# First attention of a six-stage transformer block: score banks, bank of sums and the planner's costs

## The chip, the cores and the metric

The kernel runs on one core of a Trainium2 chip. A core has TensorE (PE, matmuls and transposes), ScalarE (ACT), VectorE (DVE), GpSimd (POOL) and SyncE (SP), which here only issues transfers. Each takes its own instructions strictly in order and waits on semaphores for the others. Matmuls write to PSUM: eight banks, each of 512 f32 values in each of 128 partitions. All other tiles lie in SBUF. The metric is the device time of one execution in microseconds (us); less is better.

## The reference

The input is four sequences of 1024 tokens with 128 features. Six sublayers follow, each added to the stream (half of it for the feed-forward kind):

```python
x = L0_attn_x
x = x + 0.5 * _L0_ffn_ref(_layernorm(x), ...)
x = x + _L0_attn_ref(_layernorm(x), ...)
x = x + 0.5 * _L0_ffn_ref(_layernorm(x), ...)
x = x + 0.5 * _L1_ffn_ref(_layernorm(x), ...)
x = x + _L1_attn_ref(_layernorm(x), ...)
x = x + 0.5 * _L1_ffn_ref(_layernorm(x), ...)
```

The change rewrites the schedule of `_L0_attn_ref`, an attention by distance with 16 heads of 8 features whose queries, keys and values are one projection:

```python
Q = (x @ W_k.T).reshape(B, S, H, dk).transpose(0, 2, 1, 3)
sq_norm = jnp.sum(Q * Q, axis=-1, keepdims=True)
dot = jnp.einsum('bhsk,bhtk->bhst', Q, Q)
squared_dist = sq_norm - 2.0 * dot + sq_norm.transpose(0, 1, 3, 2)
attn = softmax(-squared_dist * inv_sqrt_dk)
context_q = jnp.einsum('bhst,bhtk->bhsk', attn, Q)
```

`_L0_ffn_ref` is a two-layer feed-forward with gelu. `_L1_attn_ref` is a causal attention with 16 heads of 64 features. `_L1_ffn_ref` is itself two layers, each a local attention (8 heads, windows of 64 tokens, normalised and rotated queries and keys) and a gated feed-forward; it runs twice.

## The kernel before

The six stages are recorded as `ffn0a`, `attn0`, `ffn0b`, `ffn1a`, `attn1`, `ffn1b`. Each stage hands the planner small steps with `at(t, f)`: a step is a function that issues a few instructions, and `t` a rough due time. Nothing is issued at once. `Plan.run` first calls every step in recording mode, in which `issue` notes each instruction's engine, its `cost` and the tiles it touches. `prepare` builds the dependences, `order` then places all steps by their ready times and priorities (it keeps one free time for each engine), and `latest` walks back from the end to give each step a new priority. `best_order` does this six times and keeps the order with the earliest end. The steps are then issued for good in that order, and `follow` ties each engine's instructions to it. Hence a changed cost in the planner can move instructions in every stage. All instructions of the kernel are issued from one line of `issue`, so every row of the profile says L237.

Names of the trace: `wordsP` is PSUM, `wordsS`, `wordsR` and `words` are parts of SBUF. A PSUM tile is asked for with `plan.bank(tag, slots, ...)`: the slots are bank numbers at which it may begin, and a tag's tiles take them in turn.

**The first attention** (`attn0`) works on units `(b, g, c)`: batch `b` (4), group `g` of four heads (4), block `c` of 128 keys (8), and for each unit the two halves `k` of 512 queries and the two pairs `p` of heads.

- `prep` prepares half a batch: layer norm, `turn` (four f32 transposes), `project` (rounded matmuls in three parts), a split of Q into three bf16 parts (`part1` to `part3`, `square`, `norm`, `spread`), and `turn_q` / `keep_q`: eight bf16 transposes into a bank and two DVE copies out of it. Batch `b + 1` is prepared while batch `b` is attended.
- `score(n)`: two matmuls with 64 rows each into a place of two banks (1024 f32 columns); two places, banks 0-1 and 2-3.
- `exp(n)`: one ACT exponential over the 1024 columns into a tile `e`, of which there are six. There are 512 of them in the stage.
- `weigh(j)`: four matmuls that add the exponentials, times Q and a column of ones, into a bank of sums; four heads lie in it 32 partitions apart. Each is f32 and runs as two passes, which stand as two records in the trace. Query half 0 has bank 4, half 1 bank 5.
- `collect`: one DVE copy of a bank of sums to SBUF after the eighth key block.
- `finish`: per half batch, transposes of the sums (`turn_c`), the division, a transpose (`turn_n`), the output projection and the add to `x`.

Bank 6 serves `turn`, `project` and half of `turn_q`; bank 7 the other half of `turn_q` and all of `finish`.

**The local attention** (`ffn1`, twice, two layers each, 32 tiles of 128 tokens per layer) matters too, since the planner may move its steps. Per tile: `project` (three f32-rounded matmul groups), DVE rotations (`turn_a`, `turn_b`), POOL additions (`add`), `sums` (a DVE reduction of the squares), `clip`, ACT `log` and `guess`, DVE `newton`, POOL `normalise`, PE `turn` of q and k, `score`, DVE `top` (two row maxima), eight ACT `exp`, DVE `inverse`, POOL `norm_e`, PE `turn_e`, ACT `untwist_e`, PE `weigh`, `project_out`. Steps of several tiles are interleaved. **The second attention** (`attn1`) has an order of the same kind.

## Time and profile before

| | us |
|---|---|
| median of 3 runs (3216.11 to 3220.35) | 3218.98 |
| the profiled execution | 3219.6 |
| its span | 3217.8 |
| first to last exponential of the first attention, start to start | 508.7 |
| mean granted TensorE clock, share of full speed | 0.984 |

The stages follow one another on PE with little overlap: the first exponential of the first attention starts at 87.96 us, the last at 596.64; the local attention's first scores are at 681.0; the second attention's first scores at 1402.3; the second local attention's first scores at 2500.2; the last matmul at 3212.4.

The costliest groups of the first attention, by shape (count, then busy time and mean length of one, then idle time of its engine just before):

```profile
L237 ACT ACTIVATE wordsS<-wordsP 128x1024 f32<-128x1024 f32 x512 | 485.7, 1028 | 23.2 <-PE wordsP L237 20.7 <-ACT wordsS L237 0.7
L237 PE MATMUL wordsP<-wordsS 64*128 64x512 bf16 x1022 | 194.4, 384 | 17.0 <-ACT wordsS L237 9.0
L237 DVE COPY words<-wordsP 128x512 f32<-128x512 f32 x32 | 22.1, 690 | 87.4 <-PE wordsP L237 87.4
```

These are the exponentials, the scores and the copies of the sums. A matmul's length in the trace is modelled and overlaps the next, so what it costs is read from the distance between starts.

### The profile page before, as it was taken

Reading aid. Unit: us, or ns where it says so; the run is one execution under the profiler, and the core shown is the slowest. Engines: PE = TensorE matmul, PEld = TensorE weight load, DVE = VectorE, ACT = ScalarE, POOL = GpSimd, SP = SyncE. Lnnn points to the kernel's source line nnn. Section 1 sums busy time; section 2 is a strip of 40 time slices with the busy share of each in tenths; the row PEclk is TensorE's granted clock in tenths of the full one; section 3 lists DMA queues with packets and bytes.
Section 4 is the critical chain, followed back from the end, with each engine's and each line's share of the span. In section 5 each row is a group of like instructions: output and inputs, shape, how many; then the busy total and the mean of one; then the engine's idle time right before and its main releaser. Section 6 shows DMA issues by size and latency. Waiting matters only on the chain.

```text
span 3217.8 us, 76341 instructions
## 1 busy us (share of the span) xinstructions
PE 3029.4 (94%) x27082; PEld 2134.7 (66%) x27108; DVE 2192.4 (68%) x6641; ACT 2467.9 (77%) x6856; POOL 1451.3 (45%) x1621
## 2 busy tenths in 40 slices
PE   8999999989998999899999999999999899999978
PEld 6322222567776777677777777777777677777767
DVE  8433341467867676778788778878787777676774
ACT  6999999768868687657777777767777788686873
POOL 1000000079958585523333333333343898585870
PEclk9999999999999999899999999999999999999989
DMA  1000000022212221122222222212231322222211
GB/s 40 1 1 1 1 3 11 21 68 63 57 40 58 44 56 35 42 57 49 47 55 45 46 50 45 52 44 47 54 80 34 76 54 56 44 53 49 55 42 30
DMA packets 209427, 137.31 MB, mean 43 GB/s; under 512 B 148548, under 2 KB 164632, under 8 KB 209048
## 3 DMA queue, kind: packets, MB, share of 16 engines
q1 hardware_dynamic: 208328, 131.87, 18.1%
q8 instruction: 217, 3.56, 0.5%
q14 instruction: 162, 1.33, 0.1%
q0 software_dynamic: 720, 0.56, 0.1%
HBM read 17.58 MB, written 2.10 MB: 6 GB/s over the span
## 4 chain that ended last, share of the span: by engine, by line
PE 58%; ACT 16%; DVE 13%; issue 5%; POOL 5%; DMA 1%; SPq 1%; DVEq 0%; ACTq 0%; POOLq 0%
PE wordsP L237 58%; ACT wordsS L237 12%; DVE wordsS L237 8%; POOL wordsS L237 3%; ACT words L237 3%; DVE words L237 3%; POOL words L237 1%; SPq L237 1%; DVE wordsP L237 1%; DVE wordsR L237 1%; DMA wordsS<-wordsS 1%; ACT wordsR L237 0%; DMA words<-words 0%; ACT wordsP L237 0%; DMA wordsS<-L_attn_x 0%
## 5 line engine op out<-in xcount | busy, mean ns | idle before, releaser
L237 PE MATMUL wordsP<-wordsS 128*128 128x128 f32 (+8 forms) x12062 | 1657.9, 331 | 114.2 <-POOL wordsS L237 44.1
L237 ACT ACTIVATE wordsS<-wordsP,wordsS 128x128 f32<-128x128 f32 (+4 forms) x1952 | 921.6, 495 | 335.7 <-PE wordsP L237 204.1
L237 PEld LDWEIGHTS wordsP<-wordsS 128*128 128x128 f32 (+3 forms) x10296 | 926.0, 145 | 329.4 <-POOL wordsS L237 85.3
L237 POOL TENSOR_SCALAR wordsS<-wordsS 128x128 f32<-128x128 f32 (+7 forms) x630 | 476.1, 758 | 678.6 <-DVE wordsS L237 484.5
L237 PE MATMUL wordsP<-wordsR 128*128 128x512 f32 (+2 forms) x2592 | 718.9, 409 | 13.6 <-ACT words L237 4.1
L237 POOL TENSOR_TENSOR wordsS<-wordsS 128x512 f32<-128x512 f32 (+1 forms) x512 | 532.6, 1053 | 430.2 <-DVE wordsS L237 411.4
L237 ACT COPY wordsS<-wordsP 128x512 f32<-128x512 f32 (+4 forms) x1040 | 543.8, 541 | 170.6 <-PE wordsP L237 160.7
L237 DVE TENSOR_REDUCE wordsS<-wordsP 128x1 f32<-128x512 f32 (+4 forms) x1024 | 576.9, 582 | 70.6 <-PE wordsP L237 64.1
L237 PE MATMUL wordsP<-wordsS,words 128*64 128x64 f32 (+3 forms) x6216 | 524.0, 299 | 34.6 <-DVE words L237 12.6
L237 ACT ACTIVATE wordsS<-wordsP 128x1024 f32<-128x1024 f32 (+3 forms) x646 | 516.8, 863 | 27.1 <-PE wordsP L237 22.7
L237 PEld LDWEIGHTS wordsP<-wordsR 128*128 128x128 f32 (+1 forms) x2592 | 451.1, 191 | 115.2 <-ACT words L237 10.2
L237 PE MATMUL wordsP<-words 128*128 128x512 f32 (+3 forms) x1540 | 414.7, 375 | 13.0 <-DMA words<-W_vT 10.9
L237 ACT ACTIVATION_READ_ACCUMULATOR wordsS<-wordsP,wordsS 128x1 f32 x1792 | 397.2, 222 | 0.0
L237 DVE COPY wordsS<-wordsP 128x512 f32<-128x512 f32 (+4 forms) x444 | 238.8, 551 | 219.0 <-PE wordsP L237 213.5
L237 PEld LDWEIGHTS <-wordsS 64*128 64x128 bf16 (+1 forms) x1792 | 117.7, 95 | 390.3 <-issue 373.1
L237 PEld LDWEIGHTS wordsP<-wordsS,words 128*64 128x64 f32 (+2 forms) x5704 | 302.6, 136 | 101.5 <-issue 48.1
L237 DVE TENSOR_TENSOR wordsS<-wordsP,wordsS 128x256 f32<-128x256 f32 (+3 forms) x560 | 252.7, 463 | 161.5 <-PE wordsP L237 122.8
L237 DVE TENSOR_TENSOR words<-wordsP,wordsS 128x256 f32<-128x256 f32 (+1 forms) x448 | 227.8, 527 | 133.4 <-PE wordsP L237 87.9
L237 PEld LDWEIGHTS wordsP<-words 128*128 128x128 f32 x1540 | 247.6, 192 | 44.1 <-DMA words<-W_kT 10.9
L237 PEld LDWEIGHTS wordsP<-words,wordsS 64*64 64x64 f32 (+1 forms) x4672 | 186.8, 142 | 79.4 <-issue 54.3
L237 PE MATMUL wordsP<-words,wordsS 64*64 64x128 f32 (+1 forms) x4672 | 227.3, 279 | 8.0 <-POOL words L237 3.1
L237 ACT ACTIVATE words<-wordsP,wordsS 128x512 fp32r<-128x512 f32 (+1 forms) x192 | 131.0, 689 | 69.8 <-PE wordsP L237 67.9
(62 smaller groups left out, 2219.7 us busy)
## 6 DMA issues: line engine op xcount, KB each, us to landing
words<-words SPq DMA_DIRECT2D x648, 128.0 KB
wordsS<-words SPq DMA_DIRECT2D x88, 128.0 KB
wordsS<-wordsS SPq DMA_DIRECT2D x48, 128.0 KB
wordsS<-wordsS SPq DMA_DIRECT2D x48, 112.0 KB
wordsS<-c_rot SPq DMA_DIRECT2D x16, 256.0 KB
wordsS<-L_attn_x SPq DMA_DIRECT2D x8, 256.0 KB
words<-wordsS SPq DMA_DIRECT2D x16, 128.0 KB
out_dram<-wordsS SPq DMA_DIRECT2D x8, 256.0 KB
```

Of the source, the lines that this page charges most:

```text
L237: self.follow(engine, getattr(engine.engine, name)(*args, **kw))
```

## The change

The change has two parts.

In the first attention, the units become `(b, g, k, c)`: a query half runs through all eight key blocks before the other begins. Then only one bank of sums is in use (bank 7, tag `a0.acc`), and it is copied out every eighth `weigh` as before. The scores get a third place (banks 4-5), and everything of `prep` and `finish` that used bank 7 shares bank 6, under one tag.

```diff
-            W["acc", k] = plan.bank(f"a0.acc{k}", [4 + k])
+            W["acc"] = plan.bank("a0.acc", [7])
...
-                pb = V["pb", K, u, z] = plan.bank("a0." + "mn"[z], [6 + z], (128, 1024), BF)
+                pb = V["pb", K, u, z] = plan.bank("a0.m", [6], (128, 1024), BF)
...
         def score(n):
-            (b, g, c), k, p = units[n // 4], n // 2 % 2, n % 2
-            sc = V["s", n] = plan.bank("a0.s", [0, 2], (128, 2, 512))
+            (b, g, k, c), p = units[n // 2], n % 2
+            sc = V["s", n] = plan.bank("a0.s", [0, 2, 4], (128, 2, 512))
...
-            ve.tensor_copy(V["cu", b][:, g, 512 * k : 512 * k + 512], W["acc", k])
+            ve.tensor_copy(V["cu", b][:, g, 512 * k : 512 * k + 512], W["acc"])
...
-                pc = V["pc", K, u] = plan.bank("a0.n", [7], (128, 16, 32))
+                pc = V["pc", K, u] = plan.bank("a0.m", [6], (128, 16, 32))
...
-        units = [(b, g, c) for b in range(self.B) for g in range(4) for c in range(8)]
-        N = 4 * len(units)
+        units = [(b, g, k, c) for b in range(self.B) for g in range(4) for k in range(2) for c in range(8)]
+        N = 2 * len(units)
```

`merge3`, `turn_n` and `output` move from `a0.n` to `a0.m` in the same way.

In the planner, the estimates change. A matmul's cost now depends on the part of the array that it uses, a switch of that part between two matmuls is charged, a change of ACT's table is charged, steps that use the SBUF port common to DVE and POOL are kept apart in the estimate, and a transfer takes longer to issue and to land.

```diff
+    TABLE = 1.3
...
+    def mode(name, args):
+
+        if name == "transpose":
+            return 128, 128, False
+        tile = lambda n: 32 if n <= 32 else 64 if n <= 64 else 128
+        return tile(args[1].shape[0]), tile(free_size(args[1])), args[1].dtype == FR
+
+    def switch(self, old, new):
+
+        if old is None or old[:2] == new[:2]:
+            return 0.0
+        return 0.2 if any(m == (64, 128, True) for m in (old, new)) else 0.1
+
+    def port(self, key, name, out, ins):
+
+        if key == "G":
+            return True
+        psum = lambda x: x.tensor.name in self.owner and self.owner[x.tensor.name].space == "P"
+        if key != "D" or psum(out) or any(psum(x) for x in ins):
+            return False
+        if name in ("tensor_tensor", "scalar_tensor_tensor"):
+            return True
+        return name in ("tensor_scalar", "tensor_copy") and free_size(out) > 1
...
-                t = 4 * free_size(x) / 2400
+                t = 4 * free_size(x) / 2400 + 0.009
+            elif x.dtype == FR:
+                t = max(free_size(x) / 2400 + 0.015, 0.112)
             else:
-                t = max(free_size(x) / 2400, 0.107 if x.dtype == FR else 0.056)
-            row = math.prod(out.tensor.shape[1:])
-            return 0.04 if free_size(w) <= 64 and out.offset // row else t + 0.004
+                t = free_size(x) / 2400 + 0.003
+
+            return t * mode[0] * mode[1] / 128**2
...
+            if s.table is not None and s.table != table:
+                t, table = max(t, free[z]) + self.TABLE, s.table
...
+                if e == "P":
+                    t, mode = t + self.switch(mode, m), m
...
+                if port:
+                    for a, b in taken_port["G" if e == "D" else "D"]:
+                        if a <= t < b:
+                            t = b
+                    taken_port[e].append((t, t + cost))
                 if e == "S":
-                    free[e] = t + 0.6
+                    free[e] = t + 0.74
                     dma = max(dma, t + 1.25) + max(cost, 0.18)
-                    end = dma + 0.96 - self.X_LAT
+                    end = dma + 1.96 - self.X_LAT
```

When a step takes its PSUM or SBUF place, all tags that share a cell with any of its tag's slots (`g.peers`) are woken, not only those of the slot taken. `latest` uses the same 0.74 for SyncE. No instruction of the other stages is added, removed or altered; they may stand in another order.

## Prediction

> **What bounds the kernel now.** I read the busy shares first, then a table by stage, then single instructions in the stage that the change rewrites, then who waited for whom.
>
> ```profile
> span 3217.8 us, 76341 instructions
> ...
> PE 3029.4 (94%) x27082; PEld 2134.7 (66%) x27108; DVE 2192.4 (68%) x6641; ACT 2467.9 (77%) x6856; POOL 1451.3 (45%) x1621
> ```
>
> TensorE (PE) looks like the bound, but ends of matmuls are modelled, so the stages decide. The rows below are the first attention, a first layer and part of a second layer of the local-attention block, and the middle of the second attention; the columns after the length are busy time of PE, weight loads, VectorE (DVE), ScalarE (ACT), GpSimd (POOL), then granted clock and DMA.
>
> ```profile
> 88.00:597.00 509.00, 488.85 (x3734) 135.88 (x3732) 161.06 (x480) 487.68 (x522) 3.26 (x3) 1.00 0.01 3
> 667.00:920.00 253.00, 231.93 (x2631) 179.40 (x2634) 195.18 (x589) 205.23 (x744) 216.10 (x219) 0.99 0.27 60
> 994.00:1150.00 156.00, 144.27 (x1590) 115.95 (x1593) 106.96 (x310) 117.01 (x415) 108.39 (x109) 0.99 0.23 51
> 1500.00:2400.00 900.00, 893.91 (x6665) 686.92 (x6663) 724.40 (x2127) 662.55 (x1899) 329.81 (x451) 1.00 0.23 51
> ```
>
> The second attention is full of matmuls (893.91 of 900). The local-attention layers fill no engine. In the first attention PE and ACT are both near 96%, so I went to single instructions, ACT and then PE.
>
> ```profile
> 262.01 2.85 ACT L237 ACTIVATE wordsS<-wordsP 128x1024 f32<-128x1024 f32 x3
> 265.10 3.77 ACT L237 ACTIVATE wordsS<-wordsP 128x1024 f32<-128x1024 f32 x4 [0.23 <-PE wordsP L237]
> ```
> ```profile
> 262.76 0.62 PE L237 MATMUL wordsP<-wordsS,words 128*128 128x128 bf16 x8
> 263.31 3.30 PE L237 MATMUL wordsP<-wordsS 64*128 64x512 bf16 x24
> 266.54 0.62 PE L237 MATMUL wordsP<-wordsS,words 128*128 128x128 bf16 x8
> 267.09 1.36 PE L237 MATMUL wordsP<-wordsS 64*128 64x512 bf16 x10
> ```
>
> One exponential is 1.02 us and a free run of them starts one every 0.915 us ((3.77 - 1.02) / 3 = 0.917, (2.85 - 1.02) / 2 = 0.915). From 263.31 to 266.54 PE did four pairs of score matmuls and two groups of sums (24 records): 3.23 us for four exponentials, 0.81 each. A block of eight transposes then adds 0.55. So ACT is the slower engine by 0.1 us each, unless other PE work comes between. The first exponential starts at 87.96 and the last at 596.64: 508.7 us for 511 steps. At 0.915 they would be 467.6, so **41.1 us of ACT's time is lost** inside this stage. In the list of single instructions a score starts 0.05 us after the exponential that frees its place, and that place's exponential can start 0.49 us after the score. With two places the next exponential (0.915) covers that with 0.915 - 0.54 = 0.37 us to spare. A group of sums holds PE 0.94 us (0.414 to its second pass, 0.525 to the score after it), so PE is late again and again; in no case of a late exponential was the score waiting for its place.
>
> ```profile
> PE wordsP L237 <- POOL wordsS L237: 44.4, 49, 5.2
> PE wordsP L237 <- ACT wordsS L237: 36.7, 90, 2.1
> PE wordsP L237 <- DVE wordsS L237: 28.3, 30, 7.7
> PE wordsP L237 <- DVE words L237: 16.9, 12, 6.4
> ```
>
> PE's own waits over the whole span: the largest, 44.4 us, is for GpSimd's normalised weights, which are turned (`turn_e`) in the local-attention layers. Followed back in a second layer:
>
> ```profile
> 1216.53 1.02 DVE L237 TENSOR_TENSOR wordsS<-wordsP,wordsS 128x512 f32<-128x512 f32 x2 [0.24 <-ACT words L237]
> ...
> 1217.73 1.23 DVE L237 TENSOR_REDUCE wordsP<-words 128x16 f32<-128x1024 f32 x1
> 1218.87 0.68 DVE L237 TENSOR_REDUCE wordsS<-wordsP 128x4 f32<-128x512 f32 x1
> ```
> ```profile
> 1219.65 0.37 ACT L237 ACTIVATE wordsS<-wordsP,wordsS 128x128 f32<-128x128 f32 x1 [1.10 <-DVE wordsS L237]
> ```
>
> Here the scores' last matmul started at 1216.4, yet their row maximum (0.68) began at 1218.87, behind a `sums` of 1.23 us for a later tile; ACT stood idle 1.10 us for it. Over 56 tiles of the second layers the median delay from scores to maximum is 1.7 us, from scores to `turn_e` 8.85, while PE's own order holds 7.6 us of work between the two.
>
> **The change, part by part.** The trace ran 3219.6 us (span 3217.8 and 1.8 around it), 0.6 above the median 3218.98; the sum is made against 3219.6.
>
> *Three score places.* One more exponential covers PE: its spare lateness grows from 0.37 to 0.37 + 0.915 = 1.29 us. I ran a sum along the scores in the order they stand: PE's work since the last score (from rows as above) minus 0.915, never below nothing, and what passes the spare time is ACT's loss. For the order before with 0.37 it gives a loss of 53 us where 41.1 is measured, so it overstates by a quarter. For the order of the changed kernel with 1.29 it gives 9.4. PE has 445 us of work between first and last score in both orders, below 467.6, so ACT stays the bound. 467.6 + 9.4 = 477, and 2 for what follows: 479, **-30 us** (508.7 - 479). Bounds: -41 if nothing is lost; -19 if four copies of sums come late as they did before (3.6, 3.2, 4.4 and 4.6 us after the last matmul, against 0.66) and PE, which now has one bank, stands for 3 us each.
>
> *One bank of sums.* Each of 32 groups of (batch, four heads, query half) ends in a copy of the bank, and the next group's first matmul waits. From the last sums matmul's start: 0.66 to the copy, 0.69 for it, 0.07 back: 1.42. Behind that wait on PE stand the scores, then ACT. The new order puts 0.89 to 1.33 us of scores and transposes behind the last pass of 0.52 us, 1.41 to 1.85 in all, except six groups with 0.92; five of these are in the last batch, where PE has only 22 of 29.3 us of work per 32 exponentials and loses nothing. Hidden; without this cover 32 x 0.9 = 29 us. "PSUM — Partial Sum Buffer" of the Trainium skill, section "PSUM bank collisions raise a hardware error", says that two engines must not use one bank at once, so matmuls cannot run on into the next group during the copy; this speaks against one bank, and by it with no filling the three places would gain about nothing. The new order fills the gap, so I side with the rows.
>
> *One bank for preparing and finishing.* `turn_q` and `finish` give up bank 7. A block's two reading copies (0.42 each, 0.34 apart) free the bank 1.0 us after its last transpose; the order leaves 1.3 to 1.7 us at all but four places (at most 1 us short each). 0, at worst +3.
>
> *The planner.* Counted along the two orders, switches of the array's row and column split are 1500 before and 1495 after; one costs 0.525 - 0.414 = 0.11 us, so -0.5. Table loads are 18 and 18. SyncE keeps 619 of 644 steps in order, and PE never waits for a transfer after the start, so the longer transfers are worth 0. PE's work summed along either order is the same within 0.3 us. In the second attention the order differs but PE has no more work and little idle: 0, within 5 either way. For the common port the trace has one row of weight:
>
> ```profile
> 440.51 3.11 DVE L237 TENSOR_TENSOR words<-words 128x64 f32<-128x64 f32 x1
> ```
>
> The same operation takes 0.45 at 444.01; GpSimd ran two additions of 1.27 from 440.99 to 443.5, and this one ended just after them. This loss (2.7 us) can go; it is within the bounds above.
>
> *What the planner moves in second layers.* There the order of PE and GpSimd is unchanged. VectorE's differs: the maxima stand before `sums` and one of the rotations, 1.2 us earlier by VectorE's own work, and three exponentials stand before the copies of the tile before. That can take up to the 44.4 us of PE's wait for GpSimd. The other end: `sums` now comes 1.3 us later (two maxima of 0.6 to 0.68), and its tile's normalising could become late: 64 tiles x 1.3 = +83 if all of it showed, but it stood before a wait of 1 to 2 us for ACT, so I take +20 as the far end. Nearest is the row with a wait really seen; but behind it stand waits of 36.7 and 28.3 us that take its place: a third, **-15**. First layers: GpSimd is 216 of 253 us busy, 0.
>
> Sum: 3219.6 - 30 - 0.5 - 15 = 3174, said as **3175**.
>
> **Rivals.** *The first attention alone*: the waits in the local layers only change hands. 3219.6 - 30 = 3190. For it: four waits of like size stand behind one another. Against: the maximum is plainly queued behind work that nobody needs yet. *Both in full*: nine tenths of 41.1 and five sixths of 44.4, -37 each: 3146. For it: the second layers fill no engine (PE 144 of 156 modelled, 7.5 us of work in a tile of 9.0). Against: it needs every other wait to stay covered. *Slower, by the late `sums`*: in the local layers `sums`, the logarithm, `newton` and `normalise` of a tile come after its neighbour's maxima; if GpSimd then starts `normalise` late, the turning of q and k waits in all 128 tiles. It decides from 30 / 128 = 0.23 us a tile; at 0.4 it gives 3219.6 - 30 + 51 = 3241. For it: GpSimd is the fullest engine of the first layers. Against: GpSimd's order hardly moved. *It does not do what it says*: one bank of sums takes back what the third place gives, 29 of 30, and the planner moves nothing: 3219.
>
> **How the numbers follow.** Forecast 0.45, first attention alone 0.22, both in full 0.16, slower 0.11, nothing 0.06. About 0.2% (6.4 us) is what can be told from no change. Faster holds the first three and a little of the last: 0.84; same 0.05; slower 0.11. The range runs from 3142 (both in full) to 3212 (the late copies, +5 in the second attention, and some loss in the local layers); the forecast's own is 3160 to 3190.
>
> **What would show it.** The exponentials' first to last start should fall to about 479 us and ACT's wait for PE there below 10; the copies of sums should start 0.66 us after the last matmul in nearly all groups. The switches and PE's summed work stay. In second layers the median from scores to maximum should fall below 1 us, and PE's wait for GpSimd from 44 to some 25. I am wrong if PE is seen waiting for VectorE at the 32 group ends, or if waits for `turn` of q and k grow by as much as those for `turn_e` fall.

## The result, and the profile after

The changed kernel takes 3224.76 us (3220.54 to 3229.07) against 3218.98 (3215.11 to 3222.05) beside it on the same chip: a ratio of 1.0018, 95% interval 1.0011 to 1.0026. It is 0.18% slower: the interval leaves out 1, but the step is smaller than the 0.2% that the prediction took as what can be told from no change. 1.4% less was forecast.

The busy shares of the changed kernel say nothing of it; every engine has what it had before:

```profile
span 3220.4 us, 76369 instructions
...
PE 3017.7 (94%) x27108; PEld 2127.8 (66%) x27108; DVE 2181.8 (68%) x6640; ACT 2460.3 (76%) x6856; POOL 1453.2 (45%) x1621
```

So again by stages. The rows of the changed kernel are: the first attention from its first to its last exponential, the first local-attention block from its first to its last score, the seam from there to the first score of the second attention, the second attention from first to last score, and the second local block likewise. Columns as before, after the length: PE, weight loads, DVE, ACT, POOL, granted clock, DMA share and GB/s.

```profile
88.60:580.90 492.30, 479.34 (x3756) 129.94 (x3756) 162.31 (x479) 478.87 (x525) 3.27 (x3) 1.00 0.01 3
666.20:1330.90 664.70, 605.72 (x6842) 481.94 (x6845) 477.57 (x1425) 515.46 (x1861) 494.77 (x498) 0.97 0.23 52
1330.90:1393.40 62.50, 51.72 (x350) 41.61 (x343) 45.20 (x149) 28.38 (x69) 13.51 (x23) 0.91 0.20 47
1393.40:2469.70 1076.30, 1065.11 (x7924) 819.02 (x7922) 855.62 (x2535) 792.55 (x2275) 394.10 (x538) 1.00 0.22 50
2494.70:3148.80 654.10, 584.26 (x6675) 464.27 (x6675) 462.34 (x1405) 503.66 (x1844) 495.04 (x499) 0.96 0.23 51
```

The same stages took 508.7, 665.9, 55.4, 1073.7 and 646.5 us before. The seam and the second local block of the kernel before, whose rows stand nowhere above:

```profile
1346.90:1402.30 55.40, 48.76 (x350) 39.76 (x343) 43.56 (x147) 28.27 (x69) 13.52 (x23) 0.98 0.21 49
2500.20:3146.70 646.50, 583.65 (x6666) 461.94 (x6675) 465.35 (x1407) 503.77 (x1849) 494.76 (x499) 0.96 0.23 52
```

The first attention gives 16.4; the seam takes 7.1, the second attention 2.6 and the second local block 7.6. What the first attention gained was lost again in stages that the diff does not touch, and the seam's clock, 0.98 before, is 0.91. PE's waits over the whole span did not shrink but changed hands (44.4 for POOL, 36.7 for ACT and 28.3 for DVE before):

```profile
PE wordsP L240 <- POOL wordsS L240: 50.6, 44, 5.2
PE wordsP L240 <- DVE wordsS L240: 34.4, 30, 6.8
PE wordsP L240 <- DVE words L240: 22.5, 19, 7.4
PE wordsP L240 <- POOL words L240: 22.3, 14, 6.5
PE wordsP L240 <- ACT wordsS L240: 19.5, 41, 1.9
```

**A second layer of the changed kernel.** In single instructions, the place that answers to the one shown before:

```profile
1198.69 1.10 PE L240 MATMUL wordsP<-words,wordsS 64*64 64x128 f32 x32
...
1200.21 0.68 DVE L240 TENSOR_REDUCE wordsS<-wordsP 128x4 f32<-128x512 f32 x1
...
1201.67 0.68 DVE L240 TENSOR_REDUCE wordsS<-wordsP 128x4 f32<-128x512 f32 x1
...
1202.46 1.23 DVE L240 TENSOR_REDUCE wordsP<-words 128x16 f32<-128x1024 f32 x1
1202.53 1.59 ACT L240 COPY wordsS<-wordsP 128x512 f32<-128x512 f32 x3
...
1204.43 0.44 ACT L240 ACTIVATE wordsS<-wordsP,wordsS 128x128 f32<-128x128 f32 x1
```
```profile
1207.25 1.04 POOL L240 TENSOR_TENSOR wordsS<-wordsS 128x512 f32<-128x512 f32 x1 [1.66 <-DVE wordsS L240]
```

Both maxima of the tile (0.68) now run before `sums` (1.23), the first 0.4 us after the last score: the move the prediction read from the order took place. But ACT then copies four banks of other tiles (1202.53 to 1204.6) before the second half's exponentials, and `inverse` of that half stands on DVE at 1207.00 behind two rotations; so POOL gets its input late and PE turns the weights as late as before. Over the 56 tiles the median from scores to the first maximum fell from 1.7 to 0.14 and 0.19 us in the two blocks, and from scores to `turn_e` it stayed (8.85 before, 8.85 and 8.88).

**One bank of sums.** 28 of the 32 copies of the bank start 0.66 us after the last matmul's start (four at 1.21 to 1.76), and the next group's first matmul starts 0 to 0.67 us after the copy's end. That step held.

**Where the first attention still loses.** 24.7 us are left above the 467.6 of a free run. In windows of 32 exponentials (29.28 at 0.915 each) the first takes 35.6 and those at the three changes of batch 33.2 to 34.0: together 19.2 too many. At the first two changes of batch ACT waits 3.1 us each for PE, and PE is not standing but busy with other matmuls (33.11 of 33.50 us, 33.06 of 33.20). At the third ACT waits only 0.6 us and has nine other instructions of its own between the exponentials. The first and the third change:

```profile
213.00:246.50 33.50, 33.11 (x250) 9.96 (x249) 17.76 (x58) 30.39 (x33) 0.00 (x0) 1.00 0.00 1
460.00:494.00 34.00, 34.00 (x256) 10.48 (x254) 15.09 (x59) 33.26 (x43) 0.00 (x0) 1.00 0.00 1
```

Counted in the trace between one exponential's start and the next, about 16 of the 24.7 us pass while ACT waits for a busy PE, 6 go to other instructions of ACT and 3 pass while PE stands idle. (PE's ends are modelled, so the split is rough.) The largest single loss, in the first window, is one where PE stands:

```profile
99.31 0.69 DVE L240 CAST wordsR<-wordsP 128x512 fp32r<-128x512 f32 x1
...
100.03 0.69 DVE L240 TENSOR_TENSOR wordsR<-wordsP,wordsR 128x512 fp32r<-128x512 f32 x1
...
100.78 0.55 PE L240 MATMUL wordsP<-wordsR 128*128 128x128 f32 x3 [2.59 <-DVE wordsR L240]
...
101.75 1.02 ACT L240 ACTIVATE wordsS<-wordsP 128x1024 f32<-128x1024 f32 x1 [1.80 <-PE wordsP L240]
```

PE stands 2.59 us at a projection of the next batch whose input DVE splits late; the score that ACT needs is queued behind it (101.26). A third place covers a PE that is busy 1.29 us too long, not one that stands for 2.59.

**The common port.** The planner now counts it, yet the one heavy case of before (3.11 us at 440.51) is there unchanged in the changed kernel:

```profile
425.44 3.14 DVE L240 TENSOR_TENSOR words<-words 128x64 f32<-128x64 f32 x1
```
```profile
425.93 2.51 POOL L240 TENSOR_TENSOR wordsS<-wordsS 128x512 f32<-128x512 f32 x2
```

"SBUF — State Buffer" of the Trainium skill, section "SBUF: two separate sides", calls the pair that DVE and GpSimd share an exclusive lock that the first comer holds for its whole instruction. The row fits a loser that stands still: DVE ends 0.14 us after the second addition. But DVE began 0.49 us before the first addition and waited out both; GpSimd had been issuing a transfer since 425.14, so the row does not settle who came first.

**The seam.** PE, DVE and POOL of the changed kernel where the seam first loses time:

```profile
1358.30 2.42 DVE L240 SCALAR_TENSOR_TENSOR wordsS<-wordsS 128x4 f32<-128x4 f32 x2
```
```profile
1358.16 2.54 POOL L240 TENSOR_TENSOR wordsS<-wordsS,words 128x512 f32<-128x512 f32 x2 [5.11 <-DMA wordsS<-wordsS]
```
```profile
1363.62 0.96 PE L240 MATMUL wordsP<-wordsR 128*128 128x512 f32 x3 [3.00 <-DVE wordsS L240]
1365.37 1.65 PE L240 MATMUL wordsP<-wordsR 128*128 128x512 f32 x3 [0.78 <-DVE wordsS L240]
```

and the granted clock there (the third number from the end of each row):

```profile
1363.00:1366.00 3.00, 1.60 (x5) 1.02 (x6) 2.92 (x16) 0.00 (x0) 0.00 (x0) 0.85 0.00 0
1366.00:1369.00 3.00, 2.22 (x6) 1.30 (x5) 2.21 (x9) 0.00 (x0) 0.00 (x0) 0.50 0.00 0
1369.00:1372.00 3.00, 3.00 (x10) 2.15 (x9) 1.48 (x5) 0.94 (x5) 2.12 (x5) 0.51 0.32 44
```

Two DVE steps on 4 elements (0.16 us each elsewhere) take 2.42 while POOL adds, then statistics of another tile stand ahead of the copy that PE needs. PE idles 3.00 us, the clock falls to 0.50 for six microseconds, and the same three matmuls take 1.65 instead of 0.96. This order pays for its hole twice; the last section shows that the hole's length alone does not decide it.

### The profile page after: what moved, and what is told of

It reads as the page before. It is cut to its first block, busy times and chain, and to the rows that moved or that the text cites. A ratio compares the mean times of both kernels' runs of the same rounds, so it can differ in the third digit from the quotient of the medians.

```text
span 3220.4 us, 76369 instructions
## 1 busy us (share of the span) xinstructions
PE 3017.7 (94%) x27108; PEld 2127.8 (66%) x27108; DVE 2181.8 (68%) x6640; ACT 2460.3 (76%) x6856; POOL 1453.2 (45%) x1621
## 4 chain that ended last, share of the span: by engine, by line
PE 68%; DVE 12%; ACT 11%; POOL 4%; issue 3%; DMA 1%; SPq 0%; DVEq 0%; ACTq 0%; POOLq 0%
PE wordsP L240 68%; ACT wordsS L240 8%; DVE wordsS L240 7%; DVE words L240 3%; POOL wordsS L240 3%; ACT words L240 3%; POOL words L240 1%; DVE wordsP L240 1%; DVE wordsR L240 1%; SPq L240 0%; ACT wordsR L240 0%; DMA words<-words 0%; DMA wordsS<-wordsS 0%; DMA words<-L_ffn_w 0%; ACT wordsP L240 0%
## 5 line engine op out<-in xcount | busy, mean ns | idle before, releaser
L240 PE MATMUL wordsP<-wordsS 128*128 128x128 f32 (+8 forms) x12088 | 1633.8, 330 | 105.1 <-POOL wordsS L240 50.6
L240 PE MATMUL wordsP<-wordsR 128*128 128x512 f32 (+2 forms) x2592 | 730.0, 413 | 21.4 <-DVE wordsR L240 6.5
L240 PE MATMUL wordsP<-wordsS,words 128*64 128x64 f32 (+3 forms) x6216 | 526.0, 300 | 47.4 <-POOL words L240 19.2
L240 ACT ACTIVATE wordsS<-wordsP 128x1024 f32<-128x1024 f32 (+3 forms) x646 | 508.4, 989 | 20.3 <-PE wordsP L240 18.0
L240 PEld LDWEIGHTS <-wordsS 64*128 64x128 bf16 (+1 forms) x1792 | 108.6, 95 | 346.2 <-issue 330.1
L240 PEld LDWEIGHTS wordsP<-words 128*128 128x128 f32 x1540 | 246.0, 191 | 50.3 <-ACT wordsS L240 14.7
L240 ACT ACTIVATE words<-wordsP 128x512 f32<-128x512 f32 x256 | 144.5, 606 | 52.0 <-PE wordsP L240 38.3
```

What stands on the lines that cost most here:

```text
L240: self.follow(engine, getattr(engine.engine, name)(*args, **kw))
```

## The experiments

The table is the yardstick for all kernels. Stages are from one profiled execution each, cut as above; "rest" is the time from the last exponential of the first attention to the last matmul, and the last column the median of the runs. "Plan later" names the new costs that act on the stages after the first attention: "mm" the matmul and switch costs, "long" the longer transfers. mix and mix_up have all new costs for the first attention alone, mix_rev has none for it.

| kernel | plan later | first attention | local a | seam | second attention | local b | rest | median |
|---|---|---|---|---|---|---|---|---|
| before | | 508.7 | 665.9 | 55.4 | 1073.7 | 646.5 | 2615.8 | 3219.0 |
| nudge_lat | | 508.8 | 656.1 | 58.3 | 1073.7 | 641.2 | 2606.3 | 3208.0 |
| a0_only | | 515.2 | 661.8 | 57.5 | 1073.6 | 646.1 | 2618.8 | 3232.4 |
| mix | | 490.0 | 664.2 | 57.5 | 1075.5 | 647.8 | 2623.9 | 3203.5 |
| mix_up | | 492.1 | 656.7 | 58.4 | 1074.4 | 640.0 | 2611.0 | 3198.9 |
| b_mm | mm | 517.7 | 657.7 | 54.7 | 1080.2 | 630.8 | 2604.7 | 3220.3 |
| mm_only | mm | 491.4 | 657.5 | 55.3 | 1078.6 | 632.9 | 2607.0 | 3190.5 |
| mm_up | mm | 489.8 | 660.2 | 58.2 | 1077.3 | 637.6 | 2616.3 | 3194.6 |
| mm_port | mm, port | 491.8 | 660.5 | 60.2 | 1075.8 | 640.2 | 2613.8 | 3194.8 |
| no_long | mm, port, tables | 493.3 | 664.1 | 57.3 | 1077.0 | 636.9 | 2618.4 | 3203.7 |
| mm_land | mm, half of long | 492.9 | 666.2 | 57.4 | 1081.0 | 637.9 | 2625.2 | 3215.1 |
| mm_issue | mm, half of long | 489.8 | 672.9 | 56.7 | 1079.1 | 636.9 | 2628.3 | 3207.4 |
| mm_long | mm, long | 492.9 | 666.3 | 60.3 | 1079.6 | 640.6 | 2625.5 | 3212.9 |
| plan_only | all | 517.0 | 664.2 | 59.1 | 1074.8 | 649.3 | 2625.3 | 3240.8 |
| after | all | 492.3 | 664.7 | 62.5 | 1076.3 | 654.1 | 2633.7 | 3224.8 |
| a_up | all | 492.5 | 664.5 | 62.1 | 1072.4 | 654.1 | 2635.5 | 3223.7 |
| mix_rev | all | 517.7 | 666.3 | 60.7 | 1076.1 | 653.5 | 2636.0 | 3249.7 |
| two_places | all | 525.2 | 664.0 | 65.3 | 1080.2 | 653.8 | 2639.5 | 3258.2 |
| b_long | long | 508.7 | 680.6 | 63.1 | 1072.3 | 660.2 | 2650.5 | 3252.8 |
| old_mm | long, port, tables | 517.8 | 684.5 | 60.4 | 1072.4 | 659.2 | 2653.4 | 3265.1 |

**First: which half of the change loses?** Three theories stood at the start. P: the planner's new costs lose in the later stages what the first attention gains. S: the gain is swallowed at the seams between stages. C: any new order moves the later stages by chance.

*a0_only*: the planner of before, the first attention of the changed kernel.

```diff
-            sc = V["s", n] = plan.bank("a0.s", [0, 2], (128, 2, 512))
+            sc = V["s", n] = plan.bank("a0.s", [0, 2, 4], (128, 2, 512))
...
-                    W["acc", k][32 * z : 32 * z + 9, :],
+                    W["acc"][32 * z : 32 * z + 9, :],
```

> The planner of before with the first attention of the change. Theory P (the planner's new costs lose what the first attention gains): the exponentials of the first attention still take about 492 us instead of 508.7, and nothing is lost behind them: about 3219 - 16 = 3203. Theory S (the gain is lost at the seams between stages whatever the planner believes): the second attention's first scores come 9 us earlier than before, not 16, and the time is 3215 to 3220. Theory C (any new order moves the later stages by chance): 3203, within 10 either way.

*plan_only*: the changed planner, the first attention of before (the same lines the other way, against the changed kernel).

> The planner of the change with the first attention of before. Theory P: the later stages lose some 18 us as in the changed kernel: about 3237. Theory S: 3217 to 3222, since without an earlier first attention there is nothing to lose at the seams. Theory C: anywhere from 3210 to 3235.

*nudge_lat*: the kernel before with one number of the planner moved by 2%.

```diff
-    X_LAT, LAT, AHEAD = 0.22, {"D": 0.13, "A": 0.09, "G": 0.09, "S": 0.22}, 0.1
+    X_LAT, LAT, AHEAD = 0.225, {"D": 0.13, "A": 0.09, "G": 0.09, "S": 0.22}, 0.1
```

> Before, with one guess of the planner (the latency between engines) moved from 0.22 to 0.225 us, which says nothing new about the chip. Theory C: stages move by 5 us or more in either direction, since another order is drawn. Theory P: every stage stays within 2 us and the time within 3 us of before.

*no_long*: the changed kernel with the old transfer estimates.

```diff
-                    free[e] = t + 0.74
+                    free[e] = t + 0.6
...
-                    end = dma + 1.96 - self.X_LAT
+                    end = dma + 0.96 - self.X_LAT
...
-            free[z] = last - 0.74 if z == "S" else start
+            free[z] = last - 0.6 if z == "S" else start
```

> The changed kernel with the old estimates for transfers (0.6 us to issue, 0.96 to land). If the longer transfers make the later stages slow (Theory P, that term): some 10 us of the 18 come back, about 3213. If not: within 3 us of 3224.8. Theory C: 3215 to 3235.

Measured: a0_only 3232.36 (ratio 1.0041, 1.0026 to 1.0055), plan_only 3240.75 (1.0067, 1.0052 to 1.0082), nudge_lat 3207.98 (0.9965, 0.9952 to 0.9978), no_long 3203.71 (0.9955, 0.9941 to 0.997). Each half alone is slower than the kernel before, in the first attention itself (515.2 and 517.0 us against 508.7), and only together do they give 492.3. A nudge without information moves a local block by 9.8 us, so chance is real and single pairs of about ten us prove nothing. But no_long beats both kernels, and that took one estimate. Of the theories' numbers, P has plan_only (3237) but not the reason, for 8.3 of what that kernel loses lie in the first attention; on a0_only P and C both said 3203 and missed by 29; on no_long P (3213) asked for too little and C (3215 or more) missed. C alone fits nudge_lat.

**Second: the costs by stage, and the third place by itself.**

*mix* and *mix_rev*: the new costs only for steps due before 575 on the plan's clock (the first attention), or only for those after.

```diff
+    def new(self, s):
+
+        return s.t < 575.0
...
-                    t, mode = t + self.switch(mode, m), m
+                    t, mode = t + (self.switch(mode, m) if self.new(s) else 0.0), m
...
-                    end = dma + 1.96 - self.X_LAT
+                    end = dma + (1.96 if self.new(s) else 0.96) - self.X_LAT
```

> Same arithmetic as the changed kernel. The new costs (array modes and switches, common port, table loads, longer transfers) are used only for steps due before 575 on the plan's own clock, which is nearly all of the first attention; every later step has the costs of before. The measure is the time from the last exponential of the first attention to the last matmul: 2615.8 us before, 2633.7 in the changed kernel (+17.9). Theory P (the new costs order the later stages worse, systematically): the first attention keeps its 492 us, the rest comes back to 2613 to 2619, 3200 to 3208 in all. Theory C (each new order draws some loss or gain of about ten us in the later stages, whatever the costs): the rest lies anywhere from 2606 to 2634, and it need not be below that of mix_rev. Third, H (a first attention that ends earlier cannot be used, because the later stages wait for something fixed in time): the rest grows by what the first attention gains, 2630 to 2634, and the time is 3217 to 3223.

> Same arithmetic as the changed kernel, with its three score places and one bank of sums. The old costs are used for steps due before 575 on the plan's clock, the new ones after that. First attention: with the old costs it took 515 us from first to last exponential in a0_only, so 512 to 518 here. Theory P: the rest takes what it takes in the changed kernel, 2628 to 2640, together 3236 to 3250. Theory C: the rest anywhere from 2606 to 2634; a rest at or below 2620 with the new costs speaks against P. Theory H: the first attention ends late, so the rest gives back: 2612 to 2618.

*a_up*: the changed kernel with `X_LAT` at 0.225.

> The changed kernel with one number of the plan moved by 2%, without any new information in it: the latency between engines 0.225 instead of 0.22 us. Theory P: the costs are the same, so the stages are too: rest 2629 to 2638, time 3220 to 3229. Theory C: at least one of the three stages after the first attention moves by 5 us or more against the changed kernel, and the time lands anywhere from 3200 to 3232.

*two_places*: the changed kernel with two places.

```diff
-            sc = V["s", n] = plan.bank("a0.s", [0, 2, 4], (128, 2, 512))
+            sc = V["s", n] = plan.bank("a0.s", [0, 2], (128, 2, 512))
```

> The changed kernel with two score places instead of three; one bank of sums, the new plan costs and everything else as in the changed kernel. If the third place is what took 16 us out of the first attention, its exponentials take 507 to 520 us from first to last here (508.7 before, 492.3 changed). If the new matmul and switch costs alone gave it, they stay at 490 to 497. If one bank of sums costs something that only the third place hides, they go above 520.

Measured: mix 3203.54 (0.9943, 0.9929 to 0.9958), mix_rev 3249.71 (1.0085, 1.007 to 1.01), a_up 3223.65 (1.0013, 1.0003 to 1.0023), two_places 3258.22 (1.0116, 1.0101 to 1.0131). S fell with a0_only and plan_only, which lie above its bounds, and H falls with mix: the last exponential comes 22.1 us earlier and 14.0 of them arrive at the end. mix and mix_rev land in P's times (3200 to 3208, 3236 to 3250), and mix_rev's rest of 2636.0 lies in P's bounds and just outside C's. But mix's rest, 2623.9, is above the 2613 to 2619 that P gave and inside C's, and a_up repeats the changed kernel's loss in seam and local b (62.1 and 654.1), where C asked for a stage that moves by 5 us: the second attention moved by 3.9, the others of the table by 0.4 at most. The first attention of two_places:

```profile
92.10:617.30 525.20, 493.19 (x3744) 137.22 (x3747) 163.49 (x486) 492.74 (x524) 3.25 (x3) 1.00 0.01 3
```

525.2 against 492.3 with three: the third place is worth 33 us beside one bank of sums. Two places and two banks take 517.0 by the same plan (plan_only), so one bank without the third place costs 8.2, together with the other order of the units and the shared bank 6, which were not tried apart. The nudges moved this stage by 2.1 us at most.

**Third: which of the costs?** L says it is the longer transfers that order the later stages worse, M that it is the matmul and switch costs.

*b_long*: the kernel before with the long transfers alone (the three lines of no_long the other way).

> The kernel before with one part of the plan's change alone: transfers are taken as longer (0.74 us to issue and 1.96 us to land, in place of 0.6 and 0.96). Theory L (the longer transfers are what orders the later stages worse): against before, the seam from the local attention to the second attention grows by 3 to 7 us, the last block by 3 to 10, the first attention within 3; 3225 to 3237. Rival M (it is the matmul and switch costs): the later stages stay within 3 each, 3216 to 3223. Theory C (chance): no sign can be told, 3208 to 3235.

*mm_only*: the changed kernel with only the matmul and switch costs; against no_long:

```diff
-    TABLE = 1.3
+    TABLE = 0.0
...
-                t, table = max(t, free[z]) + self.TABLE, s.table
+                table = s.table
...
-                if port:
+                if False:
```

> The changed kernel with only the matmul costs and the switches of the array left of the plan's new costs: no table loads, no common port, transfers as before. Theory L: as no_long, first attention 488 to 495 us, the rest 2613 to 2623, 3195 to 3208. Rival M: the rest as in the changed kernel, 2628 or more, 3215 to 3230. If the common port or the table loads matter to the first attention, its exponentials take 497 or more.

*old_mm*: the changed kernel with the matmul costs of before and no switches.

```diff
-                t = max(free_size(x) / 2400 + 0.015, 0.112)
...
-            return t * mode[0] * mode[1] / 128**2
+                t = max(free_size(x) / 2400, 0.107 if x.dtype == FR else 0.056)
+            row = math.prod(out.tensor.shape[1:])
+            return 0.04 if free_size(w) <= 64 and out.offset // row else t + 0.004
...
-                    t, mode = t + self.switch(mode, m), m
+                    mode = m
```

> The changed kernel with the matmul costs of before and no switches counted; the common port, table loads and longer transfers stay. Theory L: the first attention as in a0_only and mix_rev, 512 to 519 us, because three places pay only with an order planned by true matmul times; the later stages keep the changed kernel's loss (seam +4 to +8, last block +3 to +10), 3242 to 3256. Rival M: first attention 512 to 519, later stages as before within 3 each, 3224 to 3232. If the first attention stays at 490 to 497, the matmul costs are not what the third place needed.

*mix_up*: mix with `X_LAT` at 0.225.

> The mix kernel (new costs for the first attention, old ones after it) with the latency between engines at 0.225 instead of 0.22 us, which took 9.8 us from the first and 5.2 from the second local-attention block in nudge_lat. Theory L: the first attention within 3 of mix, and the later stages carry over what the nudge gave before: 3188 to 3197. Theory C: that gain belonged to one order and does not carry over: 3195 to 3215.

Measured: b_long 3252.82 (1.0098, 1.0081 to 1.0114), mm_only 3190.53 (0.9902, 0.9888 to 0.9917), old_mm 3265.11 (1.0142, 1.0122 to 1.0161), mix_up 3198.86 (0.9932, 0.9917 to 0.9946). b_long loses more than L gave, 33.4 us, and old_mm too; mm_only, the fastest of all, gains more than L gave. M missed all three times. mix_up lies 2 us above L's bound and within C's: what a nudge gave one order does not all carry over. The stages of b_long that lost, local a, seam, local b:

```profile
682.30:1362.90 680.60, 614.17 (x6846) 483.78 (x6845) 481.84 (x1426) 512.37 (x1861) 495.36 (x498) 0.97 0.23 51
1362.90:1426.00 63.10, 53.35 (x353) 42.34 (x343) 44.84 (x150) 28.61 (x69) 13.45 (x23) 0.88 0.20 47
2522.30:3182.50 660.20, 588.64 (x6678) 462.22 (x6675) 466.06 (x1406) 500.96 (x1847) 495.35 (x498) 0.96 0.23 51
```

The engines' work is that of before within 1% outside the seam; the 36.1 us (14.7, 7.7 and 13.7) are order and, in the seam, the clock. And after the first 100 us PE waits 0.2 us in all for transfers before, and not at all in b_long. Other engines do wait for transfers, first before, then in b_long:

```profile
POOL wordsS L237 <- DMA wordsS<-wordsS: 139.5, 11, 30.3
DVE wordsS L237 <- DMA wordsS<-wordsS: 55.3, 12, 6.7
```
```profile
POOL wordsS L237 <- DMA wordsS<-wordsS: 139.4, 12, 29.4
DVE wordsS L237 <- DMA wordsS<-wordsS: 57.5, 13, 5.5
```

These waits hardly change, so the 33 us are not time spent waiting for transfers. Transfers are not off the path altogether, though: after the first 100 us the chain that ended last passes through 37 us of them in the kernel before and through 16 in the changed kernel, which is planned with the long ones.

**Fourth: the same on the good order, the size of chance, and the two halves of "long".**

*b_mm*: the kernel before planned as mm_only (its first attention unchanged). *mm_long*: mm_only with the long transfers. *mm_port*: mm_only with the port. *mm_up*: mm_only with `X_LAT` at 0.225.

```diff
-                if False:
+                if port:
```

> The kernel before, with its two score places and two banks of sums, planned with the new matmul costs and switches alone (as mm_only, without the changed first attention). If the third place is worth what the prediction took for it, the first attention takes 20 to 35 us longer than in mm_only (491.4 us from first to last exponential), 511 to 526, and the later stages are as in mm_only within 8: 3205 to 3228. If the matmul costs alone give both gains: first attention 488 to 498, 3186 to 3200. If the later gain of mm_only belongs to its first attention and not to the costs, the rest stays at 2612 or more and the time at 3218 or more.

> mm_only with the longer transfers put back (0.74 us to issue, 1.96 to land), without table loads and common port. Theory L: they cost 15 to 35 us as in the two pairs so far (+33 on the kernel before, +21 from no_long to the changed kernel), most of it in the local-attention blocks and the seam: 3205 to 3225, first attention within 4 of mm_only. Theory C (each order draws its own loss): anywhere from 3180 to 3210; a time below 3198 ends theory L.

> mm_only with the common port put back, without table loads and longer transfers. no_long, which has the table loads as well, took 13 us more than mm_only. If the common port is the cost: 3200 to 3207. If it is the table loads: 3187 to 3195. If the port model did what it is for, VectorE's stretched steps (40 of them with 29 us of excess in no_long) would fall to half or fewer here; the prediction counted on the largest, 2.7 us, being gone.

> mm_only with the latency between engines at 0.225 instead of 0.22: the measure of chance for this order. The same step took 11 us from the kernel before, 1 from the changed kernel and 5 from mix. Theory L: within 11 of mm_only, 3180 to 3201. If it lands at 3205 or above, differences of 13 us between plans are not to be told from chance.

*mm_land* and *mm_issue*: mm_only with only the later landing, or only the longer issue.

```diff
-                    end = dma + 0.96 - self.X_LAT
+                    end = dma + 1.96 - self.X_LAT
```

> mm_only with the later landing alone: the plan takes a transfer to be there 1.0 us later (1.96 in place of 0.96), its issue stays at 0.6. mm_long lost 22.3 us with both. If the landing is the cause, as it is what the plan's due times are pulled forward by: 3205 to 3218, with 5 or more lost in each local-attention block or the seam before the second attention. If the issue is the cause: 3186 to 3197. Chance moves this order by some 4 us (mm_up, mm_port).

> mm_only with the longer issue alone (0.74 us instead of 0.6), landing as before. If the landing is the cause of mm_long's loss: 3186 to 3197. If the issue is: 3205 to 3218. If the two only hurt together, both kernels stay below 3200.

Measured: b_mm 3220.34 (1.0006, 0.9996 to 1.0016), mm_long 3212.86 (0.9981, 0.9971 to 0.999), mm_port 3194.84 (0.9925, 0.9911 to 0.994), mm_up 3194.61 (0.9926, 0.9911 to 0.9941), mm_land 3215.06 (0.9983, 0.9974 to 0.9993), mm_issue 3207.38 (0.9958, 0.9941 to 0.9974). Long transfers cost 22.3 us here, the landing alone 24.5, the issue alone 16.9: either half is enough, and they do not add. Nor does the loss sit in one place: against mm_only, local a loses 8.7 in mm_land and 15.4 in mm_issue and local b 5.0 and 4.0, while from no_long to the changed kernel local a loses 0.6 and local b 17.2. Nudges moved orders by -11.0, -1.1, -4.7 and +4.1 us (four only, all the same number moved the same way); the port's +4.3 is within that. The table loads are left with about 9 (no_long against mm_port, 3203.71 - 3194.84), which is not clear of chance either. mm_port's stretched DVE steps are as many as without it (36 against 38, about 30 us of excess against 29): that cost does not do what it is for.

One place where an order planned with long transfers differs is the end of the seam. First the changed kernel, then mm_only, at the same place of the program:

```profile
1384.20 0.69 DVE L240 TENSOR_TENSOR wordsS<-wordsP,wordsS 128x512 f32<-128x512 f32 x1 [3.01 <-PE wordsP L240]
...
1384.92 0.69 DVE L240 SCALAR_TENSOR_TENSOR wordsS<-wordsS 128x512 f32<-128x512 f32 x1
1385.53 0.74 DVE L240 SCALAR_TENSOR_TENSOR wordsR<-wordsS,wordsR 128x512 fp32r<-128x512 f32 x1
1386.20 0.74 DVE L240 SCALAR_TENSOR_TENSOR words<-wordsP,wordsS,words 128x512 fp32r<-128x512 f32 x1
...
1386.99 0.97 PE L240 MATMUL wordsP<-wordsR 128*128 128x512 f32 x3 [2.83 <-DVE words L240]
```
```profile
1371.58 0.75 DVE L240 SCALAR_TENSOR_TENSOR wordsR<-wordsS,wordsR 128x512 fp32r<-128x512 f32 x1 [2.68 <-ACT wordsR L240]
...
1372.25 0.74 DVE L240 SCALAR_TENSOR_TENSOR words<-wordsP,wordsS,words 128x512 fp32r<-128x512 f32 x1
1372.91 0.68 DVE L240 TENSOR_TENSOR wordsS<-wordsP,wordsS 128x512 f32<-128x512 f32 x1
...
1373.05 0.96 PE L240 MATMUL wordsP<-wordsR 128*128 128x512 f32 x3 [1.17 <-DVE words L240]
```

The step that frees PE's bank (`words<-wordsP,wordsS,words`, 0.74) stands fourth in the one and second in the other, behind or ahead of `collect` and `residual` (the two steps that write only `wordsS`), for which PE does not wait here. PE stands 2.83 or 1.17 us. Of the eight kernels planned with both halves of "long", seven have 2.8 us as the seam's longest wait for DVE `words`; in the twelve others it is 1.6, once 2.0. This place explains little of the loss: it is worth some 1.2 us and what the clock adds, and old_mm, the slowest of all, and mm_land and mm_issue lose without it.

The new way of waking tags is in every kernel made from the changed one and in b_mm, and was not tried alone; b_long loses without it.

## Why the prediction was wrong

**The step that failed** is "PE never waits for a transfer after the start, so the longer transfers are worth 0". The premise is right for PE itself: after the first 100 us PE waits at most 0.7 us in all for transfers, in any of the twenty kernels. The conclusion is not: in this kernel an estimate is not a time but a key by which all steps are sorted, and it can move steps without any wait for a transfer growing. Undoing it gains 21.1 us (after to no_long), adding it costs 33.4 (before to b_long) and 22.3 (mm_only to mm_long), in five pairs with its halves always the same sign and always more than any of the four nudges moved. Sorted by it, the rest of the twenty plans falls into two groups that do not overlap: 2604.7 to 2623.9 without, 2625.2 to 2653.4 with it or half of it, though the edges nearly touch. That the estimate costs this much is shown by these pairs; how it does so is not. Why a later landing puts `collect` ahead of a step that frees a bank, inside the planner's walk back from the end, and which moved steps cost the most in the local blocks, was not followed and stays open.

**Three score places, -30.** The mechanism was right, the sum was not that of this trace: 492.3 where 479 was said, -16.4. Two things were mixed in the term. The sum took the lost time from PE's work and gave 9.4 + 2; the trace has 24.7, of which 19.2 in the first window and at the three changes of batch. PE's work itself was sized too small (some 16 us of ACT's waits for a busy PE), and ACT's other instructions (6) and PE's stands (3) were not in it. The same sum had been too large for the order before, 53 for 41.1, so it was no measure to some ten us. And the term compared with a first attention planned by the old costs: by the new ones the old attention takes 517.7, and against that the new one is worth 26.3 in its stage and 29.8 in all (b_mm 3220.34, mm_only 3190.53). The gain needs the new matmul costs; with the old ones, three places take 515.2 to 517.8, in all three kernels that have them, more than two places before. The prediction read PE's order of the changed kernel and so had this in its sum without naming it. ACT's wait for PE in the stage fell from 20.7 to 13.7, not below 10.

**One bank of sums, hidden**: held, by the starts of the copies. That it is free only beside the third place is what two_places suggests, 8.2 us dearer than two banks; but PE waits only 1.7 us for the copies there, so the wait at the bank that the prediction feared was not seen.

**Second layers, -15**: fell. The maxima did come first, and median delays to them shrank as said, but `turn_e` did not come earlier. PE's wait for GpSimd went from 44.4 to 50.6, where some 25 was forecast. The term's own warning, that other waits take its place, was the whole of it, not two thirds. Nor do the matmul costs give it elsewhere: without long transfers, the mean rest of the five plans with them is 2612.0, of the five with the old ones 2615.2: the second local block gains 8.6 on average, the second attention gives back 3.6.

**Switches and port**: -0.5 can't be told; the 2.7 us of the one stretched step "can go" did not go.

**The rivals**: "does not do what it says" (3219) came nearest in time, with another mechanism: the first attention does gain, and the planner takes it back. The range was too narrow since every term for the later stages was priced as a change of one wait, and none as a new draw of the order; nudges alone move the time by up to 11 us. The three terms account for the miss: 13.6 too much for the third place, 15 for the second layers and 21.1 for the longer transfers make 49.7 of the 49.8 us between 3175 and 3224.8. So close a sum is partly luck, since each order scatters by some us. (The range's lower end, 3142, was said to be "both in full", for which the prediction's own sum gives 3146.)

## What to carry to other kernels

A cost in a list scheduler is a sorting key: changing it can make the program slower without any wait for what it prices growing (how near the new transfer figures are to the truth was not measured). So change one cost at a time, and nudge a meaningless number to learn how far orders scatter before believing a difference. A buffer more pays only if the order is planned to use it: here the new first attention lost 6 to 9 us by the old matmul costs and gained 15 to 19 by the new. mm_only, the changed kernel without table loads, port and longer transfers, is the version to keep: 3190.53, 1.0% below the kernel before (interval 0.8 to 1.1%).

## What was not expected of the hardware

The clock: PE busy for 2.62 of 5 us and then idle until 1363.62 was enough for a granted clock of 0.50 over six microseconds. In mm_only, where PE's longest wait in the seam was 1.56 us, the clock stayed at 1.00. But the length of one stand does not decide. The kernel before has stands of 1.34 and 1.56 us at the end of its seam and falls to 0.50; the changed kernel stands 2.69 us in a local layer after a busy stretch and keeps 1.00 (first row before, second changed):

```profile
1399.60:1402.30 2.70, 1.42 (x3) 1.12 (x4) 1.23 (x2) 1.73 (x2) 0.00 (x0) 0.51 0.69 153
```
```profile
830.20:834.00 3.80, 3.43 (x30) 2.79 (x32) 3.47 (x19) 3.01 (x14) 3.80 (x5) 1.00 0.35 77
```

PE had been busy for 1.98 of the 3.6 us ahead of the first (1396.0 to 1399.6) and for 3.44 of the 3.5 us ahead of the second's stand (824.0 to 827.5). What decides was not tested. "TensorE: Matmul & The Clock Gate" of the Trainium skill, section "Why this matters for your kernels", warns of idle gaps over about 3 us; the 3.00 here is at that edge, the kernel before drops after stands of half that length, and in the changed kernel the rows from 1388 to 1394, after a stand of 2.83 us, have a clock of 0.59.

The port: a DVE step on 4 elements, 0.16 us elsewhere, took up to 1.3 when POOL added 128x512 values beside it. In the changed kernel 39 DVE steps are 0.3 us or more above the median of their own kind, about 30 us in all (47 and about 35 before), and every one of them ran beside an instruction of POOL. Of 22 two-input steps on 4 elements that started while POOL worked on 128x512 values, 21 took over 0.4 us.
